# Two transformer layers on one core: the banks of the block products, weight places in halves, the fold of the weights, and the first loads

## The chip, the cores and the metric

The kernel runs on one core of one Trainium2 chip. The metric is the device time of one execution in microseconds (us). The engines of the core are PE (matrix products), PEld (PE's weight loads), DVE (vector), ACT (activations), POOL (GpSimd) and SP, which here issues every DMA. Each engine runs its own list of instructions in order, and semaphores tie the lists together.

## The reference

Two layers follow each other on `x` (16 batches of 256 rows by 256), all in float32. Each layer is self attention, cross attention and a feed-forward part, each with a layer norm that is scaled and shifted by a projection of the condition. Cut to what matters:

```python
# layer 0: 16 heads of 64 (rotary positions), width 1024; layer 1: 16 heads of 16, width 256
def layer(x, cond, context):
    h = norm(x) * (1 + cond @ g1) + cond @ b1
    x = x + attention(h, h)              # softmax(q k^T / sqrt(dh)) v, then @ wo
    h = norm(x) * (1 + cond @ g1) + cond @ b1   # layer 1 has its own three sets
    x = x + attention(h, norm(context))  # layer 1: context without the norm
    h = norm(x) * (1 + cond @ g2) + cond @ b2
    return x + gelu(h @ w1) @ w2         # 256 -> 1024 -> 256
```

The context has 256 rows by 192. In layer 1 the condition passes a silu first.

## The kernel before

The work is six phases (`p` = 0 to 5): self attention, cross attention and feed-forward of layer 0, then the same of layer 1. Each phase goes over 16 batches; a batch in a phase is a job. An attention job has two steps (`s` = 0, 1), a feed-forward job four. One loop over all steps issues everything, and the order in which a line of it stands in the program is the order on each engine; nothing is rescheduled. `x` stays in SBUF for all batches.

The PSUM has eight banks. In a layer 0 attention step the order on PE is:

- `stage_rotary` (L474) for the next step: the products of hT and cT with `wk` and `wq`. Unit e of the two uses banks 2e and 2e+1. DVE multiplies them by the rotary tables (`m`, L490), POOL combines these to `qk` (L498). A unit's `m` tiles have two places for each of two tags, so the second unit's `m` waits for POOL.
- `layer0_sums` (L594, products at L602): the weighted sums of the two units, in banks 4 and 5. ACT copies each bank to `raw` (L609).
- for `s` = 1, `finish_folded` (L702): the output projection of the batch before (`late`). It is one level of a block scheme with seven products of half-size blocks instead of eight; the blocks' sums of the hidden side are made in `fold_inner` (L693), those of the weights, once a phase, in `fold_weights` (L678). The products went to banks 1 and 0, DVE adds them to `x` in five instructions (L714 to L721).
- `layer0_values` (L424): the values of the next batch, in banks 6 and 7, copied out by ACT (L442).
- `scores` (L813), `stage_s` (L520): the score products of the next step, one unit in banks 0 to 3, then one in banks 4 to 7 (L533). ACT makes the exponentials (`pr`, L545) from them.
- for a cross attention step to come, `start_keys` (L462, product at L469), which reads `wk` for the step after.

DVE in a step adds the exponentials (`both`, L554), turns them (L560) and sums them (L567). In the next step `sum_up` (L569) sends the sums through DRAM to spread them (L579, L582); POOL multiplies `raw` with them (`scale`, L591) and makes three of the five hidden blocks' sums (L700), DVE the other two. Between the last `both` and the first of the next step DVE also prepares the norm of a batch to come.

The tiles of weights have places by tag: `wk`, `wq`, `wv`, `wo`, each with one place but `wo`. A phase's weights are fetched into them by `load_phase` (L789), in parts: "early" at batch 1 or 3 of the phase before, "values" at the start of that phase's last batch, "keys" at the end of the first step of that batch, after which `scores` calls `start_keys` on them. SP issues DMAs in the order of the program and stands still where one has to wait.

`idle_products` (L136) multiplies the identity with itself at the start, before the condition has been fetched.

Of the kernel before, what the change touches and what calls it, by code (L numbers as in the profile page):

```python
# [16 lines left out]
P = 128  # L17
N = 256
# [25 lines left out]
def fast(ctx: ExitStack, tc: tile.TileContext, a: dict, out: bass.AP, flag):  # L44
# [79 lines left out]
    nc.sync.dma_start(out=cond, in_=a["cond_1024"])  # L124
    load_x(0)
    nc.sync.dma_start(out=rows, in_=a["rows"])

    condT = const.tile([P, 2, KC, NB], F32, name="condT")
# [7 lines left out]
    def idle_products(n):  # L136

        for _ in range(n):
            nc.tensor.matmul(bank(0, P), ident, ident, start=True, stop=True)

    sig = work.tile([NB, D], F32, tag="inv", name="sig")
    nc.scalar.activation(sig, cond, AF.Sigmoid)
    soon = stat.tile([NB, 1], F32, tag="ve", name="soon")
    nc.scalar.activation(soon, cond[:, 0:1], AF.Exp)
    silu = work.tile([NB, D], F32, tag="inv", name="silu")
    idle_products(2)
    transpose_condition(0, cond)
    nc.vector.tensor_mul(silu, sig, cond)
    idle_products(2)
    transpose_condition(1, silu)  # L150
    idle_products(2)
    pr = bank(4, n_rows)
    nc.tensor.transpose(pr, rows, ident[:n_rows, :n_rows])
    idle_products(1)

    def load_modulation(shift_w, scale_w, name):
        w = wpool.tile([P, KC, 2, D], F32, tag="mod", name=f"mod_{name}", bufs=1)
        nc.sync.dma_start(out=w[:, :, 0, :], in_=shift_w.rearrange("(c p) m -> p c m", p=P))
        nc.sync.dma_start(out=w[:, :, 1, :], in_=scale_w.rearrange("(c p) m -> p c m", p=P))
        return w  # L160
# [23 lines left out]

    def layer0_modulation(i):
        w = load_modulation(a[f"L0_xcond_b{i}_w"], a[f"L0_xcond_g{i}_w"], f"a{i}")
        return lambda at: modulation(
            f"a{i}", at, 0, w,
            *(row_of[f"L0_xcond_{n}"][0] for n in (f"ln{i}_w", f"ln{i}_b", f"b{i}_b", f"g{i}_b")),
        )  # L190
# [23 lines left out]


    def load_layer0_attention(kind, part, between=None):
        halves = [slice(i * 512, (i + 1) * 512) for i in range(4)]
        wkv_src = chunked(a[f"{kind}_wkv"])
        w = {}
        if part == "keys":  # L220
            w["wk"] = wtile([P, 2, H * 64], "wk", f"wk_{kind}")
            w["wq"] = wtile([P, KC, H * 64], "wq", f"wq_{kind}")
            for i, cut in enumerate(halves[:2]):
                nc.sync.dma_start(out=w["wk"][:, :, cut], in_=wkv_src[:, :, cut])
                nc.sync.dma_start(out=w["wq"][:, :, cut], in_=chunked(a[f"{kind}_wq"])[:, :, cut])
                if between is not None and i == 0:
                    between()
# [22 lines left out]
    def load_layer1_cross(part):  # L250
        if part != "early":
            return {}
        w = wtile([P, 3, 2, D], "wk", "wqkv_c")
        nc.sync.dma_start(out=w[:, 0], in_=chunked(a["L1_xcond_Wq"]))
        nc.sync.dma_start(out=w[:, 1], in_=chunked(a["Wk_filled"]))
        nc.sync.dma_start(out=w[:, 2], in_=chunked(a["Wv_filled"]))
        wo = wtile([P, KC, D], "wo", "wo_b2", 2)
        nc.sync.dma_start(out=wo, in_=chunked(a["L1_xcond_Woc"]))
        return {"wq": w[:, 0], "wk": w[:, 1], "wv": w[:, 2], "wo": wo,
                "bo": broadcast_row(a["L1_xcond_boc"], "bo", "bo_b2"),  # L260
                "bv": broadcast_row(a["L1_xcond_bv"], "bv", "bv_b2"),
                "bq": lambda c: column("L1_xcond_bq", c), "bk": lambda c: column("L1_xcond_bk", c)}

    def load_ffn(w1n, w2n, b1n, b2n, key, part):
        if part == "keys":
            w1 = wtile([P, KC, 4 * D], "wq", f"w1_{key}")
            nc.sync.dma_start(out=w1, in_=chunked(a[w1n]))
            return {"w1": w1}
        if part == "early":
# [192 lines left out]
    def start_keys(job, u, at):  # L462


        for g in range(2):
            for half in range(2):
                col = (2 * u + half) * P + 64 * g
                r, m = slice(64 * half, 64 * half + 64), slice(64 * g, 64 * g + 64)
                nc.tensor.matmul(  # L469
                    bank(at + half, 2, N)[m, 1, :], job["phase"]["w"]["wk"][r, 1, col : col + 64],  # L470
                    job["kT"][r, 1, :], start=True, stop=False,
                )

    def stage_rotary(job, u, half, first_bank):  # L474


        w, key, cross = job["phase"]["w"], job["key"], job["cross"]
        at = (2 * u + half) * P
        pq = bank(first_bank + half, 2, N)
        for k in range(1 if cross else 2):  # L480
            product(
                pq[:, 1, :], w["wk"][:, k, at : at + P], job["kT"][:, k, :],
                k == 0 and not cross, k == 1 or cross,
            )
        for k in range(2):
            product(pq[:, 0, :], w["wq"][:, k, at : at + P], job["hT"][:, k, :], k == 0, k == 1)
        turns = []
# [167 lines left out]
    def ffn_hidden(job, u):  # L655
# [5 lines left out]
        for c in range(2):  # L661
            for k in range(KC):
                product(
                    ph[:, c, :], w["w1"][:, k, (2 * u + c) * P : (2 * u + c + 1) * P], job["hT"][:, k, :],
                    k == 0, k == KC - 1,
# [12 lines left out]
    def fold_weights(ph):  # L678
# [3 lines left out]
        for m, x, y, op in ((1, b[0][0], b[1][1], ALU.add), (3, b[0][1], b[1][1], ALU.subtract),  # L682
# [6 lines left out]
            else:  # L689
                folded[m] = work.tile([P, 4, P], F32, tag="qk", name=f"folded_w_{m}", bufs=4)  # L690
            (nc.gpsimd if ph["kind"] == "attn" and m < 4 else nc.vector).tensor_tensor(folded[m], x, y, op)

# [9 lines left out]
    def finish_folded(job, at):  # L702

        x, weights, hidden = xs[job["b"]], job["phase"]["folded"], job.pop("folded")
        final = job is jobs[-1]
        first, second, third = (bank(i, 4, P) for i in (at if final else (*at, at[1])))
        places = {5: first[:, 0], 2: first[:, 1], 4: first[:, 2], 3: first[:, 3],
                  1: third[:, 0], 7: second[:, 1], 6: second[:, 2]}
        for m in (3, 6, 4, 5, 2, 1, 7) if final else places:
            for c in range(4):  # L710
# [46 lines left out]
    def count_outside():  # L757
# [11 lines left out]
        {"layer": 0, "kind": "attn", "cross": False, "load": lambda part: load_layer0_attention("sa", part, load_first),  # L769
         "mod_load": lambda: layer0_modulation(1)},  # L770
        {"layer": 0, "kind": "attn", "cross": True, "load": lambda part: load_layer0_attention("ca", part), "mod_load": None},
# [59 lines left out]
    phases[0]["make_mod"] = phases[0]["mod_load"]()  # L831
    for part in ("keys", "early"):
        load_phase(0, part)
# [5 lines left out]


    jobs[0]["hraw"] = bank(7, KC, N)
    found = moments(xs[0], "first")
# [23 lines left out]
    for i, (j, s) in enumerate(steps):  # L866
# [10 lines left out]
        if s == 1 and job["b"] == (3 if ffn else 1) and more:  # L877
            load_phase(job["p"] + 1, "early")
        if s == 0 and job["b"] == NB - 1 and more:
            load_phase(job["p"] + 1, "values")  # L880
        if layer0 and not ffn and s == 1 and job["b"] == 2:
# [46 lines left out]
        elif layer0:  # L928
# [9 lines left out]
            if make_mod:  # L938
                make_mod["mod"] = make_mod["make_mod"](5)
            stage_t(job, 2 * s + 1, 1)  # L940
            rotary(then, 1, 0)
            if late is not None and s == 1:
                fold_inner(late, nc.vector, 7, 6)
            rotary(then, 1, 1)
            for e in range(2):
                layer0_sums(job, 2 * s + e, 4 + e if then else e)
# [3 lines left out]
            if late is not None and s == 1:  # L950
                finish_folded(late, (1, 0) if then else (7, 6))
            if late is not None and s == 0:
                scale(late)
                fold_inner(late, nc.gpsimd, 5, 2, 1)
            if s == 0 and job["b"] == 1:
                fold_weights(job["phase"])
            if nxt["kind"] == "attn":
# [5 lines left out]
            else:  # L963
                prepare_norm(third)
                prepare_context(third)
                prepare_input(after)
        else:
            then = attention(i + 1, 1)
# [15 lines left out]
            else:  # L984
                prepare_norm(third)
                prepare_input(after)
        if s == 0 and job["b"] == NB - 1 and more:
            load_phase(job["p"] + 1, "keys")
        scores(i + 1)
# [621 lines left out]
```

## The time and the profile before

| | us |
|---|---|
| three timed runs | 2240.68, 2245.42, 2246.43 (median 2245.42) |
| profiled execution, its own time | 2240.61 |
| its span, first to last instruction | 2238.8 |
| PE busy, share | 2192.0, 98% |
| DVE busy, share | 1721.4, 77% |
| ACT busy, share | 837.6, 37% |
| POOL busy, share | 998.4, 45% |

The profile follows one execution. "Busy" counts time in which an engine has an instruction under way; a wait is idle time of an engine just before an instruction, with what ended it. The granted clock of PE is told for a stretch of time (1.00 is full, 0.50 half). The line numbers in it are those of the code above.

By phase: the self attention of layer 0 lasts to about 660 us of the span, its cross attention to about 1330, its feed-forward part to about 1550; layer 1's two attentions follow to about 2017, and its feed-forward part to the end.

### The profile page before, as it was taken

What the parts mean: (1) busy time and instruction counts of PE and PEld (TensorE: products, weight loads), DVE (VectorE), ACT (ScalarE), POOL (GpSimd) and SP (SyncE); (2) the same over time, 40 slices, a digit from 0 to 9 for tenths busy, and PEclk for the clock granted to TensorE, in tenths of its full rate; (3) what the DMA queues carried; (4) which work ended last, traced back from release to release, by engine and by line L of the source; (5) the groups of instructions that cost most, each with busy time, mean ns of one, the idle gap of its engine ahead of it and who ended that gap; (6) DMA issues with size and microseconds to landing.
All of it is one profiled execution on the core that took longest, in us unless ns stands there. A gap on an engine that the chain in (4) does not pass through costs nothing.

```text
span 2238.8 us, 110884 instructions
## 1 busy us (share of the span) xinstructions
PE 2192.0 (98%) x50601; PEld 1446.6 (65%) x50601; DVE 1721.4 (77%) x3188; ACT 837.6 (37%) x1303; POOL 998.4 (45%) x970
## 2 busy tenths in 40 slices
PE   9999999999999899999999999999999999999998
PEld 5666666666656566666666668777656665656787
DVE  6888778788888899889988885564677777777654
ACT  2323332332332332333323332223566666663322
POOL 3656465465565566565665652211222222222120
PEclk9999999999999999999999999999999999999999
DMA  6210111111131321212212123221211232223221
GB/s 188 48 36 22 27 36 22 27 36 22 43 99 38 76 53 34 62 36 43 56 34 43 41 57 87 57 43 32 60 41 39 50 81 61 60 51 99 64 61 37
DMA packets 305703, 117.69 MB, mean 53 GB/s; under 512 B 242548, under 2 KB 288968, under 8 KB 305096
## 3 DMA queue, kind: packets, MB, share of 16 engines
q1 hardware_dynamic: 305224, 110.51, 20.6%
q8 instruction: 397, 6.50, 1.2%
q14 instruction: 82, 0.67, 0.1%
HBM read 77.14 MB, written 33.29 MB: 49 GB/s over the span
## 4 chain that ended last, share of the span: by engine, by line
PE 79%; POOL 7%; DVE 7%; DMA 3%; issue 2%; SPq 1%; ACT 0%; POOLq 0%; DVEq 0%; ACTq 0%
PE banks L82 53%; PE banks L533 14%; PE banks L602 6%; PE banks L618 5%; POOL raw L591 3%; DVE m L490 2%; POOL folded L700 2%; POOL qk L498 1%; DMA spread<-sums_seen 1%; DVE rows L567 1%; PE banks L469 1%; DMA sums_seen<-inv 1%; SPq L582 1%; DVE squares L560 1%; DVE folded L700 1%
## 5 line engine op out<-in xcount | busy, mean ns | idle before, releaser
L545 ACT ACTIVATE pr<-banks 128x1024 f32<-128x1024 f32 x576 | 487.4, 938 | 246.1 <-PE banks L533 220.9
L498 POOL TENSOR_TENSOR qk<-m,m 128x512 f32<-128x512 f32 x256 | 346.8, 1375 | 405.7 <-DVE m L490 272.3
L490 DVE TENSOR_TENSOR m<-banks,rope 128x512 f32<-128x512 f32 x512 | 325.8, 680 | 95.2 <-POOL qk L498 75.8
L554 DVE TENSOR_TENSOR both<-pr 128x512 f32<-128x512 f32 x256 | 236.7, 932 | 93.0 <-ACT pr L545 92.8
L533 PE MATMUL banks<-qk 32*64 32x256 f32 x8192 | 242.7, 379 | 21.9 <-DVE x L721 21.0
L533 PEld LDWEIGHTS banks<-qk 32*64 32x64 f32 x8192 | 192.1, 132 | 96.8 <-issue 51.5
L609 ACT COPY raw<-banks 128x512 f32<-128x512 f32 x128 | 75.1, 586 | 479.4 <-PE banks L602 479.4
L602 PE MATMUL banks<-pr,v 128*32 128x256 f32 x4096 | 233.4, 379 | 1.0 <-DVE add_a L182 1.0
L668 ACT ACTIVATE g<-banks,cols 128x256 f32<-128x256 f32 x256 | 107.0, 470 | 294.9 <-PE banks L82 275.7
L442 ACT COPY v<-banks 128x512 f32<-128x512 f32 x128 | 71.8, 587 | 336.8 <-PE banks L437 168.5
L602 PEld LDWEIGHTS banks<-pr,v 128*32 128x32 f32 x4096 | 132.9, 110 | 90.0 <-DVE add_a L182 1.5
L591 POOL TENSOR_TENSOR raw<-raw,spread 128x512 f32<-128x512 f32 x128 | 172.4, 1381 | 14.0 <-DMA spread<-sums_seen 13.3
L82 PE MATMUL banks<-folded_w,folded 128*32 128x128 f32 x5952 | 174.2, 273 | 0.0
L82 PEld LDWEIGHTS banks<-folded_w,folded 128*32 128x32 f32 x5952 | 163.9, 110 | 0.0
L560 DVE STREAM_TRANSPOSE squares<-both 128x1024 f32<-128x1024 f32 x128 | 159.4, 1246 | 4.4
L567 DVE TENSOR_REDUCE rows<-squares 128x32 f32<-128x1024 f32 x128 | 155.4, 1214 | 2.2
L653 POOL TENSOR_TENSOR oT<-oT,spread 128x256 f32<-128x256 f32 x64 | 45.7, 735 | 209.9 <-DVE spread L652 209.9
L296 POOL TENSOR_TENSOR rstd<-ve,neg_half 128x2 f32<-128x2 f32 x95 | 74.2, 781 | 142.1 <-DVE ve L294 138.8
L82 PE MATMUL banks<-hT,wk_sa 128*32 128x256 f32 x2048 | 136.4, 384 | 0.9 <-ACT hT L362 0.9
L618 PE MATMUL banks<-pr,wide_v 128*32 128x256 f32 x2048 | 134.4, 379 | 1.1 <-ACT pr L545 1.1
L700 POOL TENSOR_TENSOR folded<-raw,raw 128x512 f32<-128x512 f32 x93 | 134.0, 1467 | 2.4
L82 PE MATMUL banks<-hT,wq_sa 128*32 128x256 f32 x2048 | 134.8, 381 | 0.0
(156 smaller groups left out, 3626.2 us busy)
## 6 DMA issues: line engine op xcount, KB each, us to landing
turned<-blocks SPq DMA_DIRECT2D x380, 64.0 KB
fetched<-turned SPq DMA_DIRECT2D x380, 64.0 KB
spread<-sums_seen SPq DMA_DIRECT2D x128, 128.0 KB
x<-in_x SPq DMA_DIRECT2D x16, 256.0 KB
fetched_c<-turned_c SPq DMA_DIRECT2D x64, 64.0 KB
cT<-in_ctx_turned SPq DMA_DIRECT2D x16, 256.0 KB
out<-x SPq DMA_DIRECT2D x16, 256.0 KB
ctx<-in_ctx SPq DMA_DIRECT2D x16, 192.0 KB
```

The costliest lines, as they stand in the source:

```text
L82: nc.tensor.matmul(out[cut], lhsT[:, cut], rhs, start=start, stop=stop)
L490: nc.vector.tensor_tensor(m, pq, rope[:, s : s + 1, :].to_broadcast([P, 2, N]), ALU.mult)
L498: nc.gpsimd.tensor_tensor(r, x, y, (ALU.subtract, ALU.add)[out])
L533: nc.tensor.matmul(banks[64 * g : 64 * g + 64, at + h, t * N : (t + 1) * N], lhs, rhs, start=(half == 0), stop=(half == 1 or job["layer"] ...
L545: nc.scalar.activation(pr[:, one], sc[:, one], AF.Exp, scale=0.125 if job["layer"] == 0 else 0.25)
L554: nc.vector.tensor_tensor(job["both"][:, 2 * p : 2 * p + 2, :], pr[:, :, 0, :], pr[:, :, 1, :], ALU.add)
L560: nc.vector.transpose(job["squares"].rearrange("p b k -> p (b k)"), job.pop("both").rearrange("p h n -> p (h n)"))
L567: nc.vector.tensor_reduce(job["rows"][:, u, :], job.pop("squares"), AX.X, ALU.add)
L591: nc.gpsimd.tensor_tensor(part, part, spread[:, u : u + 1, :].to_broadcast([P, 2, N]), ALU.mult)
L602: nc.tensor.matmul(o[32 * h : 32 * h + 32, half, :], v[:, t, col : col + 32], prs[h // 2][:, h % 2, t, :], start=(t == 0), stop=(t == NT - 1),
L618: nc.tensor.matmul(o[32 * h : 32 * h + 32], v[:, t, 4 * c + h, 32 * e : 32 * e + 32], prs[h // 2][:, h % 2, t, :], start=(t == 0), stop=(t ...
L700: eng.tensor_tensor(folded[m], *sums[m])
```

## The change

- The block products of a layer 0 attention batch go to the banks of the weighted sums, 4 and 5, and no longer to 1 and 0. After the last attention step that has such products, they take three banks (7, 6, 5), in the order that only the very last batch had. The modulation that is made in such a step goes to bank 6, no longer 5.
- The places `wk` and `wq` become two places each, `wk0`, `wk1`, `wq0`, `wq1`. The first halves are fetched at the start of the last batch of a layer 0 attention phase, ahead of the values; the second halves after that step's last `stage_rotary`. The last feed-forward phase's `w1` is fetched at batch 1 of the phase before. The weights of layer 1's cross attention are laid into the new places.
- `fold_weights` of an attention phase is called at the end of the first batch (`s` = 1) and no longer in the first step of the second; all five blocks' sums are on POOL, where it was two on POOL and three on DVE.
- For the batch whose `finish_folded` falls in the last attention step, the three hidden blocks' sums that POOL made are made by DVE in that step.
- At the start `x` of batch 0 is fetched between the two halves of the modulation's weights, and the rows of vectors after them. The idle products have 256 columns in place of 128; there are five instead of seven.

The diff, cut to its core:

```diff
     def idle_products(n):
         for _ in range(n):
-            nc.tensor.matmul(bank(0, P), ident, ident, start=True, stop=True)
+            nc.tensor.matmul(
+                bank(0, 2, P), ident, ident.unsqueeze(1).to_broadcast([P, 2, P]), start=True, stop=True
+            )
...
-        if part == "keys":
-            w["wk"] = wtile([P, 2, H * 64], "wk", f"wk_{kind}")
-            w["wq"] = wtile([P, KC, H * 64], "wq", f"wq_{kind}")
...
+        if part in ("first", "last"):
+            i = ("first", "last").index(part)
+            wk, wq = (wtile([P, 2, 512], f"w{n}{i}", f"w{n}{i}_{kind}") for n in "kq")
+            nc.sync.dma_start(out=wk, in_=wkv_src[:, :, halves[i]])
+            nc.sync.dma_start(out=wq, in_=chunked(a[f"{kind}_wq"])[:, :, halves[i]])
+            w[f"wk{i}"], w[f"wq{i}"] = wk, wq
...
-            (nc.gpsimd if ph["kind"] == "attn" and m < 4 else nc.vector).tensor_tensor(folded[m], x, y, op)
+            (nc.gpsimd if ph["kind"] == "attn" else nc.vector).tensor_tensor(folded[m], x, y, op)
...
-        final = job is jobs[-1]
-        first, second, third = (bank(i, 4, P) for i in (at if final else (*at, at[1])))
+        hurry = len(at) == 3
+        first, second, third = (bank(i, 4, P) for i in (at if hurry else (*at, at[1])))
...
-        for m in (3, 6, 4, 5, 2, 1, 7) if final else places:
+        for m in (3, 6, 4, 5, 2, 1, 7) if hurry else places:
...
         if s == 1 and job["b"] == (3 if ffn else 1) and more:
             load_phase(job["p"] + 1, "early")
-        if s == 0 and job["b"] == NB - 1 and more:
-            load_phase(job["p"] + 1, "values")
+            if job["layer"] == 1:
+                for part in ("first", "last"):
+                    load_phase(job["p"] + 1, part)
+        leaving = layer0 and not ffn and job["b"] == NB - 1
+        if leaving and s == 0:
+            for part in ("first", "values"):
+                load_phase(job["p"] + 1, part)
...
             if make_mod:
-                make_mod["mod"] = make_mod["make_mod"](5)
+                make_mod["mod"] = make_mod["make_mod"](6)
             stage_t(job, 2 * s + 1, 1)
             rotary(then, 1, 0)
             if late is not None and s == 1:
-                fold_inner(late, nc.vector, 7, 6)
+                fold_inner(late, nc.vector, *((7, 6) if then else (6, 5, 2, 1, 7)))
             rotary(then, 1, 1)
+            if leaving and s == 0:
+                load_phase(job["p"] + 1, "last")
...
             if late is not None and s == 1:
-                finish_folded(late, (1, 0) if then else (7, 6))
+                finish_folded(late, (4, 5) if then else (7, 6, 5))
             if late is not None and s == 0:
                 scale(late)
-                fold_inner(late, nc.gpsimd, 5, 2, 1)
-            if s == 0 and job["b"] == 1:
-                fold_weights(job["phase"])
+                if nxt["kind"] == "attn":
+                    fold_inner(late, nc.gpsimd, 5, 2, 1)
...
                 prepare_input(after)
+                if job["b"] == 0:
+                    fold_weights(job["phase"])
...
-        if s == 0 and job["b"] == NB - 1 and more:
-            load_phase(job["p"] + 1, "keys")
         scores(i + 1)
```

More of the change, by code (lines that the diff above doesn't have):

```diff
@@ L124, in fast @@
     nc.sync.dma_start(out=cond, in_=a["cond_1024"])
-    load_x(0)
-    nc.sync.dma_start(out=rows, in_=a["rows"])
     condT = const.tile([P, 2, KC, NB], F32, name="condT")
@@ L138, in idle_products, with condition, load_modulation @@
         for _ in range(n):
-            nc.tensor.matmul(bank(0, P), ident, ident, start=True, stop=True)
[L141 to L156, printed above, removed]
+            nc.tensor.matmul(
+                bank(0, 2, P), ident, ident.unsqueeze(1).to_broadcast([P, 2, P]), start=True, stop=True
+            )
+    def condition():
+        sig = work.tile([NB, D], F32, tag="inv", name="sig")
+        nc.scalar.activation(sig, cond, AF.Sigmoid)
+        soon = stat.tile([NB, 1], F32, tag="ve", name="soon")
+        nc.scalar.activation(soon, cond[:, 0:1], AF.Exp)
+        silu = work.tile([NB, D], F32, tag="inv", name="silu")
+        idle_products(1)
+        transpose_condition(0, cond)
+        nc.vector.tensor_mul(silu, sig, cond)
+        idle_products(1)
+        transpose_condition(1, silu)
+        idle_products(2)
+        pr = bank(4, n_rows)
+        nc.tensor.transpose(pr, rows, ident[:n_rows, :n_rows])
+        idle_products(1)
+        return pr
+    def load_modulation(shift_w, scale_w, name, between=None):
         w = wpool.tile([P, KC, 2, D], F32, tag="mod", name=f"mod_{name}", bufs=1)
         nc.sync.dma_start(out=w[:, :, 0, :], in_=shift_w.rearrange("(c p) m -> p c m", p=P))
+        if between is not None:
+            between()
         nc.sync.dma_start(out=w[:, :, 1, :], in_=scale_w.rearrange("(c p) m -> p c m", p=P))
@@ L183, in modulation, with layer0_modulation @@
         return factor, addend
-    def layer0_modulation(i):
-        w = load_modulation(a[f"L0_xcond_b{i}_w"], a[f"L0_xcond_g{i}_w"], f"a{i}")
+    def layer0_modulation(i, between=None):
+        w = load_modulation(a[f"L0_xcond_b{i}_w"], a[f"L0_xcond_g{i}_w"], f"a{i}", between)
         return lambda at: modulation(
@@ L219, in load_layer0_attention @@
         w = {}
-        if part == "keys":
-            w["wk"] = wtile([P, 2, H * 64], "wk", f"wk_{kind}")
-            w["wq"] = wtile([P, KC, H * 64], "wq", f"wq_{kind}")
[L223 to L227, printed above, removed]
+        if part in ("first", "last"):
[4 more added lines that the diff above has]
+            w[f"wk{i}"], w[f"wq{i}"] = wk, wq
+            if between is not None and i == 0:
+                between()
         if part == "values":
@@ L252, in load_layer1_cross @@
             return {}
[L253 to L256, printed above, removed]
+        wqk = wtile([P, 2, 2, D], "wk0", "wqk_c")
+        nc.sync.dma_start(out=wqk[:, 0], in_=chunked(a["L1_xcond_Wq"]))
+        nc.sync.dma_start(out=wqk[:, 1], in_=chunked(a["Wk_filled"]))
+        wv = wtile([P, 2, D], "wk1", "wv_c")
+        nc.sync.dma_start(out=wv, in_=chunked(a["Wv_filled"]))
         wo = wtile([P, KC, D], "wo", "wo_b2", 2)
         nc.sync.dma_start(out=wo, in_=chunked(a["L1_xcond_Woc"]))
-        return {"wq": w[:, 0], "wk": w[:, 1], "wv": w[:, 2], "wo": wo,
+        return {"wq": wqk[:, 0], "wk": wqk[:, 1], "wv": wv, "wo": wo,
                 "bo": broadcast_row(a["L1_xcond_boc"], "bo", "bo_b2"),
@@ L264, in load_ffn @@
     def load_ffn(w1n, w2n, b1n, b2n, key, part):
[L265 to L268, printed above, removed]
+        if part in ("first", "last"):
+            i = ("first", "last").index(part)
+            w1 = wtile([P, KC, 2 * D], f"wq{i}", f"w1{i}_{key}")
+            nc.sync.dma_start(out=w1, in_=chunked(a[w1n])[:, :, i * 2 * D : (i + 1) * 2 * D])
+            return {f"w1{i}": w1}
         if part == "early":
@@ L466, in start_keys @@
             for half in range(2):
-                col = (2 * u + half) * P + 64 * g
+                col = (2 * (u % 2) + half) * P + 64 * g
                 r, m = slice(64 * half, 64 * half + 64), slice(64 * g, 64 * g + 64)
                 nc.tensor.matmul(
-                    bank(at + half, 2, N)[m, 1, :], job["phase"]["w"]["wk"][r, 1, col : col + 64],
+                    bank(at + half, 2, N)[m, 1, :], job["phase"]["w"][f"wk{u // 2}"][r, 1, col : col + 64],
                     job["kT"][r, 1, :], start=True, stop=False,
@@ L477, in stage_rotary @@
         w, key, cross = job["phase"]["w"], job["key"], job["cross"]
-        at = (2 * u + half) * P
+        at = (2 * (u % 2) + half) * P
         pq = bank(first_bank + half, 2, N)
@@ L481, in stage_rotary @@
             product(
-                pq[:, 1, :], w["wk"][:, k, at : at + P], job["kT"][:, k, :],
+                pq[:, 1, :], w[f"wk{u // 2}"][:, k, at : at + P], job["kT"][:, k, :],
                 k == 0 and not cross, k == 1 or cross,
@@ L485, in stage_rotary @@
         for k in range(2):
-            product(pq[:, 0, :], w["wq"][:, k, at : at + P], job["hT"][:, k, :], k == 0, k == 1)
+            product(pq[:, 0, :], w[f"wq{u // 2}"][:, k, at : at + P], job["hT"][:, k, :], k == 0, k == 1)
         turns = []
@@ L663, in ffn_hidden @@
                 product(
-                    ph[:, c, :], w["w1"][:, k, (2 * u + c) * P : (2 * u + c + 1) * P], job["hT"][:, k, :],
+                    ph[:, c, :], w[f"w1{u // 2}"][:, k, (2 * (u % 2) + c) * P : (2 * (u % 2) + c + 1) * P], job["hT"][:, k, :],
                     k == 0, k == KC - 1,
@@ L769, in fast @@
         {"layer": 0, "kind": "attn", "cross": False, "load": lambda part: load_layer0_attention("sa", part, load_first),
-         "mod_load": lambda: layer0_modulation(1)},
+         "mod_load": lambda: layer0_modulation(1, lambda: load_x(0))},
         {"layer": 0, "kind": "attn", "cross": True, "load": lambda part: load_layer0_attention("ca", part), "mod_load": None},
@@ L831, in fast @@
     phases[0]["make_mod"] = phases[0]["mod_load"]()
-    for part in ("keys", "early"):
+    nc.sync.dma_start(out=rows, in_=a["rows"])
+    for part in ("first", "last", "early"):
         load_phase(0, part)
@@ L835, in fast @@
         load_x(b)
+    pr = condition()
     jobs[0]["hraw"] = bank(7, KC, N)
```

## The prediction

> **What bounds the kernel now.** First the page: PE is busy for 98% of the span, so no more than 47 us of waits are there to be had, unless PE is slow while it is busy.
>
> ```profile
> PE 2192.0 (98%) x50601; PEld 1446.6 (65%) x50601; DVE 1721.4 (77%) x3188; ACT 837.6 (37%) x1303; POOL 998.4 (45%) x970
> ```
>
> Then the list of waits, PE's lines alone (who waits, for whom: us in total, times, longest).
>
> ```profile
> PE banks L533 <- DVE x L721: 21.0, 15, 2.8
> PE banks L469 <- DMA wk_ca<-in_ca_wkv: 4.7, 1, 4.7
> PE banks L82 <- DMA w_b<-in_L_xcond_W: 3.2, 1, 3.2
> PE banks L82 <- POOL rstd_c L296: 2.3, 1, 2.3
> PE banks L82 <- POOL folded L700: 2.2, 2, 1.6
> PE banks L602 <- DVE add_a L182: 1.0, 1, 1.0
> ```
>
> The edits aim at these. The largest is the scores' wait for DVE's last addition to x. The same list over 60 to 650 us has 0.7 us of it, over 688 to 1300 us 20.4 us: it belongs to layer 0's cross attention. Whether PE gains it depends on DVE, so the third view is what DVE itself waits for in that stretch.
>
> ```profile
> DVE m L490 <- POOL qk L498: 36.6, 29, 2.5
> DVE both L554 <- ACT pr L545: 14.3, 32, 2.0
> DVE m L490 <- PE banks L82: 7.9, 15, 1.6
> ```
>
> The second and third line are DVE waiting for PE's scores and products: together 22.2 us. The first is the shape of the rotary (unit two's `m` needs POOL's `qk` of unit one) and stays. The windows (us, then busy time of PE, PEld, DVE, ACT, POOL, the granted clock of PE, DMA share and GB/s) show the steps, and PE's clock after three waits.
>
> ```profile
> 892.86:910.19 17.33, 16.25 (x338) 9.56 (x337) 15.05 (x26) 7.00 (x10) 7.90 (x8) 1.00 0.38 82
> 910.19:932.58 22.39, 22.39 (x556) 15.23 (x552) 20.98 (x33) 6.02 (x8) 17.11 (x14) 1.00 0.07 18
> 814.50:830.76 16.26, 16.26 (x341) 9.19 (x337) 13.67 (x23) 6.93 (x10) 7.78 (x8) 1.00 0.41 91
> 668.53:671.93 3.40, 3.03 (x28) 1.48 (x32) 0.00 (x0) 0.00 (x0) 3.32 (x4) 0.50 0.99 347
> 1177.11:1180.52 3.41, 3.41 (x79) 3.10 (x67) 2.22 (x6) 1.67 (x2) 1.90 (x4) 0.50 0.28 45
> 1323.89:1327.29 3.40, 3.38 (x64) 3.14 (x68) 3.40 (x4) 0.00 (x0) 2.75 (x2) 0.50 0.02 5
> ```
>
> A cross batch is a step of 17.33 and one of 22.39 us; without the wait the first would be 16.26. In the second DVE works 20.98 of 22.39 us. Last, rows of one timeline (start, us, engine, line), around one such wait.
>
> ```profile
> 919.14 1.79 DVE L554 TENSOR_TENSOR both<-pr 128x512 f32<-128x512 f32 x1
> 922.07 0.59 ACT L609 COPY raw<-banks 128x512 f32<-128x512 f32 x1 [5.99 <-PE banks L602]
> 923.55 1.93 PE L82 MATMUL banks<-wo_ca,folded 128*32 128x128 f32 x64
> 933.20 0.42 DVE L721 TENSOR_TENSOR x<-banks,x 128x256 f32<-128x256 f32 x1
> 933.77 4.43 PE L533 MATMUL banks<-qk 32*64 32x256 f32 x128 [1.19 <-DVE x L721]
> 935.87 1.94 ACT L545 ACTIVATE pr<-banks 128x1024 f32<-128x1024 f32 x2 [1.18 <-issue]
> ```
>
> **Banks 4 and 5.** Nothing is added or removed; what changes is who waits. Unit one's scores (banks 0 to 3) no longer wait for the additions; unit two's (4 to 7) do. A unit is half of 128 records in 3.71 us, so the additions get 1.86 us more. The waits, mostly 0.9 to 1.6 us, would vanish at today's DVE timing. PE would gain 20.4 us plus 1.7 us, because the half clock at 1177 follows one of these waits. But PE then runs ahead of DVE: a batch costs PE 16.26+22.39=38.65 us, and DVE 39.72 less the waits it can lose. In the batch shown these are 0.65 us on ACT and 0.28 on PE, so DVE needs 38.79. The two are nearly equal, and once PE's lead of 1.86 us is used up DVE sets the pace. Over the phase DVE can give 22.2 us; I take that. The new neighbour is the copy of bank 4, which must be out before the first block product: it ends at 922.66, the product starts at 923.55. Bank 5 is needed two rows of 1.93 us later. Both cost nothing. Late next: L721 before unit two.
>
> **The fold of the weights.** In the cross phase three DVE instructions of 1.48 us (mean of that row) go: +4.4. Five on POOL at its 1.47 (L700's row) are 7.4 us. POOL stands idle for 6.60 us between cT and its next `qk` (896.9 to 903.5), so `qk` comes 0.8 later. Beside them run DVE's `both`. Alone one takes 0.69; the row at 919.14, next to POOL's blocks' sums, took 1.79. [...] I take the trace: 4.4-2.0-0.8=+1.6. PE's 2.3 us (put down to rstd_c) lies in the same batch and is DVE's or POOL's lateness, so it isn't counted again. In the self phase DVE has cover; there it is worth the 0.7 wait and a little: 1.0.
>
> **Weights in halves.** `wk_ca` was issued at 664.4 and PE stood still for 4.7 us, then ran 3.4 us at half clock (1.7 lost, of which some 1.5 in products). PE's side: 6.2. SP's queue: two DMAs (1 MB) now pass the values, the context, the sums and four spreads; two more pass eight fetches. At the 347 GB/s of the 668.53 row, 2 MB take 6.0 us from 649.1 on, and the values are used at 657.7: a wait of 0 to 1.3. The sums' DMA stands behind them, so `spread`, which POOL already waited 3.5 us for here, comes 1 to 2 us later; then raw, blocks' sums, `qk`, and DVE's second `m`, which was at 677.9. I get 676.4 without a late spread and 677.9 with one. DVE's side thus gains 0 to 1.5: 0.7, and DVE's side counts, as the phase behind it is DVE's. Fetching `w1` a phase sooner: all of the 3.2.
>
> **Clock.** [...] By the trace the dips cost 3x1.7=5.1. I use the trace, on PE's side only.
>
> **End of the cross phase.** PE waited 1.65+0.59 for POOL's blocks' sums and then ran 3.4 us at half clock: 3.9 on PE's side. Now DVE makes five at 0.70: its `both` end near 1322.5 (3.31 for two, less the contention), the first sum at 1323.2. From there six products of 0.94 us end at 1328.9, where they ended at 1331.0: +2.1. The modulation's bank: the 1.0 us wait goes, inside DVE's pace.
>
> **First loads.** Not shown before, so bounded. Idle products: 0.61 us each for 128 columns (1.23 for two at half clock); 256 columns cost 0.61 to 1.22, five of them 3.1 to 6.1 against 4.3; I take 4.5, near the mean. The rows of vectors land after 768 KB and stand before the modulation in PE's order: up to 1.3 late. For: the first products (16 records) took 1.94 us at 11.5 and 1.04 from 16.6, half clock, 2.5 us lost; denser products may get full clock sooner. Ends -1.3 and +3.2; I take +1.0.
>
> **Sum.** 22.2+1.6+1.0+0.7+3.2+2.1+1.0=31.8. Against the profiled execution, 2240.61 (span 2238.8 and 1.8 around it), that is 2208.8: 2209. The median, 2245.42, lies 4.8 higher; the three runs spread over 5.8, so the range leans upward.
>
> **Rivals.**
> - PE sets the pace all through. For: every edit meets a PE wait. 20.4+1.7+2.3+1.0 in the cross phase, 6.2, 3.9, 3.2, start and self phase 2: 40.7, so 2200. Against: 20.98 of 22.39.
> - Contention eats the cross phase: POOL's instructions meet more of DVE's, and the wait for L721 comes back at unit two. What stays is PE's lead 1.9, half of the recoverable 22.2 lost: 2240.6-20.6 is 2220; if nearly all of it is lost, 2228.
> - Slower: the copies of banks 4 and 5 (L609) come late and hold the block products in all 31 batches. The slack is 0.89 us. To undo 31.8 us and lose 0.3% (6.7), each must wait 1.24, so the copy must come 2.1 us later than now; at 2.5 later it is 31x1.61=50 more, 2259. Against: ACT was idle 5.99 us before the copy.
> - The change does not do what it says: PE meets another wait right behind L721 (`qk`, ready 3.5 us before in the batch shown), and only loads and ends count: 2238 to 2246.
>
> **How the numbers follow.** A measurement of this kernel tells about 0.3% from no change, 6.7 us. Likeliest case 0.62 (alone 2202 to 2217); PE's pace 0.18; contention 0.12; no effect 0.05; slower 0.03. Faster: 0.62+0.18+0.12=0.92. The range reaches from below PE's pace, 2197, to 2226; left out are the slower case, no effect and the worst of contention and start, under 0.2.
>
> **What would show it.** L533's wait for L721 under 6 us in all; L469's and `w_b`'s gone; DVE's waits for `pr` and PE in the cross phase under 6 us, with the one for `qk` near 36; cross batches near 38.8 us; half clock at most once after the start. Wrong: a wait of L82 for `raw` L609, or cross batches at 39.5 with DVE without waits.

## The result and the profile after

The changed kernel takes 2213.14 us (median of four runs, 2212.19 to 2216.62) beside 2245.93 us for the kernel before (2240.68 to 2246.55): a ratio of 0.9862, with a 95% interval of 0.9843 to 0.9880. Run again beside the last two experiments it took 2211.99 us against 2242.09, 0.9864 (0.9849 to 0.9880). Its profiled execution took 2212.19 us (span 2210.4). The line numbers of the changed kernel are those of before plus 7 around the steps: L533 is now L540, L545 L552, L554 L561, L490 L497, L498 L505, L591 L598, L700 L707, L714 to L721 are L721 to L728.

The page's row of busy times, and PE's part of the list of waits (who waits, for whom: us in total, times, longest):

```profile
PE 2190.7 (99%) x50597; PEld 1431.3 (65%) x50597; DVE 1705.5 (77%) x3185; ACT 838.3 (38%) x1303; POOL 1005.2 (45%) x973
```

```profile
PE banks L82 <- DVE folded L707: 3.8, 2, 2.8
PE banks L540 <- DVE x L728: 2.2, 7, 0.3
PE banks L540 <- DVE x L724: 1.0, 3, 0.3
PE banks L82 <- ACT hT L369: 1.4, 1, 1.4
```

Of the six waits shown of before, those for `wk_ca`, `w_b`, `rstd_c` and `add_a` are gone, and the one for the last addition to `x` went from 21.0 to 2.2 us; 1.0 us of waits for the third addition (L724) is new. The one for POOL's `folded` (2.2) is now one for DVE's, and longer. DVE's own waits in the cross phase (681.3 to 1273 us):

```profile
DVE m L497 <- POOL qk L505: 47.4, 30, 4.3
DVE m L497 <- PE banks L82: 0.6, 2, 0.3
DVE both L561 <- ACT pr L552: 0.2, 1, 0.2
```

Here is the surprise. The 22.2 us that DVE spent waiting for PE and `pr` are down to 0.8, as foreseen; but the wait for POOL's `qk`, which I took as fixed at 36.6 us, is 47.4.

**A wait that the list does not show.** In this trace a hold between the two units' scores can lie partly inside a row's busy time. The timeline (start, us, engine, line) of one first step of a batch, in the changed kernel, and of the same step in the last experiment below, where nothing holds it:

```profile
1074.73 2.71 PE L540 MATMUL banks<-qk 32*64 32x256 f32 x66
1077.75 1.98 PE L540 MATMUL banks<-qk 32*64 32x256 f32 x62 [0.31 <-DVE x L728]
1079.66 1.09 PE L476 MATMUL banks<-cT,wk_ca 64*64 64x256 f32 x16
```

```profile
1074.08 3.86 PE L555 MATMUL banks<-qk 32*64 32x256 f32 x128
1077.86 1.09 PE L491 MATMUL banks<-cT,wk_ca 64*64 64x256 f32 x16
```

From the first score product to the first product of another kind it is 4.93 us in the one and 3.78 in the other: 1.15 us lost where the list counts 0.31. The records of the first row reach past unit one's 64. So I count the length of the score blocks, each with the wait in front of it: over the 29 steps from the start of the cross phase, what they take above 3.64 us, the shortest, is 23.3 us before (19.4 of it in front) and 12.2 after (nothing in front). The wait moved to unit two, smaller, as "late next" had it, and did not vanish.

**Where the time went.** The starts of the same steps in both profiles give the saving by stretch (us):

| stretch | before | after | saved | foreseen |
|---|---|---|---|---|
| to the third scores | 64.11 | 61.70 | 2.4 | 1.0 (first loads) |
| to the last self attention step | 596.39 | 595.97 | 0.4 | 1.0 (fold), values 0 |
| from there to the 30th of 32 cross steps | 614.51 | 593.91 | 20.6 | 24.5 (22.2+1.6+0.7) |
| from there to the first `w_a` product | 55.80 | 53.46 | 2.3 | 2.1 |
| to the first `w_b` product | 690.89 | 688.03 | 2.9 | 3.2 |
| to the end | 217.1 | 217.3 | -0.2 | 0 |
| sum | 2238.8 | 2210.4 | 28.4 | 31.8 |

### The profile page after: what moved, and what is told of

Read it like the earlier page. It is cut to its first block, busy times and chain, and to the rows that moved or that the text cites. A ratio compares the mean times of both kernels' runs of the same rounds, so it can differ in the third digit from the quotient of the medians.

```text
span 2210.4 us, 110913 instructions
## 1 busy us (share of the span) xinstructions
PE 2190.7 (99%) x50597; PEld 1431.3 (65%) x50597; DVE 1705.5 (77%) x3185; ACT 838.3 (38%) x1303; POOL 1005.2 (45%) x973
## 4 chain that ended last, share of the span: by engine, by line
PE 91%; DVE 3%; POOL 2%; DMA 1%; issue 1%; SPq 0%; ACT 0%; DVEq 0%; POOLq 0%; ACTq 0%
PE banks L82 60%; PE banks L540 15%; PE banks L609 9%; PE banks L625 5%; PE banks L476 1%; PE banks L444 1%; DVE m L497 1%; POOL raw L598 1%; POOL qk L505 0%; DMA sums_seen<-inv 0%; POOL folded L707 0%; DMA spread<-sums_seen 0%; PE banks L175 0%; DVE both L561 0%; DVE folded L707 0%
## 5 line engine op out<-in xcount | busy, mean ns | idle before, releaser
L552 ACT ACTIVATE pr<-banks 128x1024 f32<-128x1024 f32 x576 | 488.4, 936 | 229.5 <-PE banks L540 212.1
L505 POOL TENSOR_TENSOR qk<-m,m 128x512 f32<-128x512 f32 x256 | 345.3, 1368 | 364.5 <-DVE m L497 244.8
L497 DVE TENSOR_TENSOR m<-banks,rope 128x512 f32<-128x512 f32 x512 | 325.1, 678 | 99.0 <-POOL qk L505 94.3
L561 DVE TENSOR_TENSOR both<-pr 128x512 f32<-128x512 f32 x256 | 233.4, 923 | 80.1 <-ACT pr L552 79.7
L540 PE MATMUL banks<-qk 32*64 32x256 f32 x8192 | 246.6, 378 | 3.9 <-DVE x L728 2.2
L540 PEld LDWEIGHTS banks<-qk 32*64 32x64 f32 x8192 | 184.6, 131 | 89.3 <-issue 23.0
L598 POOL TENSOR_TENSOR raw<-raw,spread 128x512 f32<-128x512 f32 x128 | 172.8, 1383 | 18.0 <-DMA spread<-sums_seen 11.4
L82 PE MATMUL banks<-hT,wq_ca 128*32 128x256 f32 x2048 | 134.0, 379 | 0.0
```

What stands on the lines that cost most here:

```text
L82: nc.tensor.matmul(out[cut], lhsT[:, cut], rhs, start=start, stop=stop)
L497: nc.vector.tensor_tensor(m, pq, rope[:, s : s + 1, :].to_broadcast([P, 2, N]), ALU.mult)
L505: nc.gpsimd.tensor_tensor(r, x, y, (ALU.subtract, ALU.add)[out])
L540: nc.tensor.matmul(banks[64 * g : 64 * g + 64, at + h, t * N : (t + 1) * N], lhs, rhs, start=(half == 0), stop=(half == 1 or job["layer"] ...
L552: nc.scalar.activation(pr[:, one], sc[:, one], AF.Exp, scale=0.125 if job["layer"] == 0 else 0.25)
L561: nc.vector.tensor_tensor(job["both"][:, 2 * p : 2 * p + 2, :], pr[:, :, 0, :], pr[:, :, 1, :], ALU.add)
```

## The experiments

Each was timed in turns with the kernel before; ratios are to that kernel. Three chips were used, on which the kernel before took 2240.5 (the first four), 2241.5 (the next four) and 2242.1 us (the last three), so times of different groups are compared by ratio or by stretches of the profile. The changed kernel itself was not run beside the first eight, and the kernel before took 2245.9 us beside its first timing: ratios of different groups can differ by some 0.2% for that alone. Differences of a few us from the changed kernel are therefore read from the profiles, of one execution each.

**Banks alone.** The kernel before, with one part of the change.

```diff
-                make_mod["mod"] = make_mod["make_mod"](5)
+                make_mod["mod"] = make_mod["make_mod"](6)
...
-                finish_folded(late, (1, 0) if then else (7, 6))
+                finish_folded(late, (4, 5) if then else (7, 6))
```

> The kernel before with one edit: block products in banks 4 and 5, the modulation in bank 6. DVE's pace (the theory): DVE's waits for pr and PE in the cross phase, 22.2 us before, nearly go, PE's wait for L721 falls from 21 to under 4, and PE is at most one unit of scores (1.9) ahead; the weights' fold stays on DVE. 18 to 21 us less than before: 2225 to 2228. PE's pace: 20.4+1.7+1.0 less, 2223, and DVE would keep idle time in every batch. If the waits only move to another place: under 8 us less, over 2238.

Measured: 2219.76 us, 0.9919 (0.9902 to 0.9936), 20.7 us less. In the profile the stretch across the cross phase is 596.41 us, 18.1 saved of the 20.6, and the score blocks lose 7.1 us in place of 23.3. Nearly the whole gain of that stretch is in two bank numbers. DVE's wait for `qk` over 681.3 to 1273 us grew only a little, from 36.6:

```profile
DVE m L490 <- POOL qk L498: 39.8, 30, 3.7
```

**Banks undone.** The changed kernel with the block products back in banks 1 and 0 and the modulation in bank 5.

> The changed kernel with the block products back in banks 1 and 0 and the modulation in bank 5 (the last step keeps its three banks). DVE's pace: DVE again waits some 20 us for pr and PE, PE some 17 us for the last addition to x; 16 to 20 us over the changed kernel: 2229 to 2233. If the other edits had made the room (a lighter DVE): under 10 over it.

Measured: 2235.23 us, 0.9974 (0.9964 to 0.9985), 2 us above the expected range. PE's waits, then DVE's in its cross phase:

```profile
PE banks L540 <- DVE x L728: 24.1, 15, 3.2
```

```profile
DVE m L497 <- POOL qk L505: 37.5, 27, 3.1
DVE both L561 <- ACT pr L552: 18.6, 30, 2.2
DVE m L497 <- PE banks L82: 7.2, 14, 1.4
```

All three old waits are back, and `qk` is at its old size. Without the banks the other edits are worth 0.26%. Six windows of 3.41 us at half clock fell into the stretch up to its 30th cross step, where before had two (granted clock 0.98 from 684.49 to 1279.25 us; before had 1.00 from 688.96 to 1275.01). But the profiled execution was the slowest of the eight (2239.61 us), so they tell why it was slow; why the median lies above the range stays open.

**Halves fetched late.** The changed kernel, first and last halves at the end of the step, where `keys` stood.

```diff
-            for part in ("first", "values"):
-                load_phase(job["p"] + 1, part)
+            load_phase(job["p"] + 1, "values")
...
-            if leaving and s == 0:
-                load_phase(job["p"] + 1, "last")
...
+        if leaving and s == 0:
+            for part in ("first", "last"):
+                load_phase(job["p"] + 1, part)
         scores(i + 1)
```

> The changed kernel with both halves of the weights fetched where the kernel before did, at the end of the last batch's first step; the places stay in halves. PE stands still at start_keys again for some 4.7 us and may fall to half clock. DVE's pace: the phase behind it is DVE's, and DVE loses only 0 to 1.5 us by the late fetch, so 0 to 2.5 us over the changed kernel: 2213 to 2216. PE's pace: the wait and the half clock come back whole, 4.7 to 6.2 more: 2218 to 2219.

Measured: 2214.37 us, 0.9893 (0.9877 to 0.9910); span 2210.3, that of the changed kernel.

```profile
PE banks L476 <- DMA wk_ca<-in_ca_wkv: 4.7, 1, 4.7
```

PE stood still for 4.7 us again, with a window at half clock (mean granted clock of the span 0.998, of the changed kernel's 0.999), and in the profile it cost nothing that lasts: across the cross phase 594.17 us against 593.91, and the score blocks lost 7.4 us in place of 12.2. What PE loses there it would otherwise have lost to DVE behind it. This speaks for "DVE's pace" and against "PE's pace" (6.2 us more). The times do not decide it: the profiled execution was the fastest of its four (2212.21 to 2217.91 us), and the ratio is 0.3% above that of the changed kernel, which was not timed beside it.

**Fold undone.** The changed kernel with `fold_weights` in the first step of the second batch, two on POOL and three on DVE.

> The changed kernel with the weights' fold where and on which engines it was (first step of batch 1, two sums on POOL, three on DVE). By the trace's contention: 1.6 in the cross phase, under 1.0 in the self phase: 1.6 to 2.6 over the changed kernel, 2215 to 2216. If each vector addition beside the five POOL instructions had waited a whole one: 2.3 less in the cross phase, so 2211 to 2212.

Measured: 2214.98 us, 0.9890 (0.9873 to 0.9906). In the profile the self phase is no longer than with the change (595.96 us against 595.97): what the kernel before lost there is won back by the banks alone, too (595.37 us, and 596.39 before). The cross stretch is 592.69 us, against 593.91, 593.06, 592.96 and 593.80 in the four profiles with the new fold: the edit brought nothing there.

Its price had been put about right. In the changed kernel, beside POOL's five sums (7.58 us), DVE's four `both` took 2.55+1.80+0.62=4.97 us, where four alone take 2.76: 2.2 lost. The prediction's 2.0 was twice what two in a row lost in the profile of before, next to POOL's `raw` (2.36 in place of 1.38):

```profile
1316.12 4.72 POOL L591 TENSOR_TENSOR raw<-raw,spread 128x512 f32<-128x512 f32 x3
1317.34 2.36 DVE L554 TENSOR_TENSOR both<-pr 128x512 f32<-128x512 f32 x2
```

The other case of the expectation, that each of the four waits for a whole sum on POOL (1.47 us by the prediction, 5.9 in all: 4.4-5.9-0.8=-2.3), did not come. The single instructions in the changed kernel:

```profile
726.23 1.71 POOL L698 TENSOR_TENSOR folded_w<-wo_ca 128x512 f32<-128x512 f32 x1
726.73 1.77 DVE L561 TENSOR_TENSOR both<-pr 128x512 f32<-128x512 f32 x1
```

The second `both` began while POOL's first sum ran, and ended 0.56 us after it; the third took 1.80 us, and ended 0.55 us after POOL's fourth. Each of the two took 1.1 us longer than the 0.69 of one alone, a little less than POOL's fourth sum lasted (1.28 us). The first, which had begun ahead of POOL's sums, took 0.86, and the fourth, behind them, 0.62. So 5.9 was too large because two of the four lost 1.1 each, the first 0.17 and the fourth nothing.

With three DVE sums of 1.47 us back, PE waited 2.3 us once for `folded` and then ran a window at half clock (mean granted clock of the span 0.998), but the score blocks lost 6.8 us in place of 12.2. As with the halves fetched late, PE lost less to DVE later; that the one makes up for the other fits both runs, and was not tested by itself.

**Start undone.** First loads and idle products as before.

> The changed kernel with the first loads in the old order and seven idle products of 128 columns. The first scores began at 26.6 us in place of 27.9, and the first step was 1.1 shorter; both come back: 1.3 to 2.4 over the changed kernel, 2214 to 2216, with the first products of rotary at half clock until about 16.6. If the clock depends on where its window falls, and not on these edits: within 1 of the changed kernel.

Measured: 2213.11 us, 0.9868 (0.9845 to 0.9890): no difference from the changed kernel's 0.9862 and 0.9864. The third scores start at 62.89 us, inside the 61.40 to 65.52 of the nine profiles with the new start.

**End undone.** The last batch's three blocks' sums on POOL again.

> The changed kernel with the last folded batch of the cross phase as before: POOL makes three of its five sums, two banks, old order. The changed kernel waits 2.77 us there for DVE, without half clock. Theory: 2.1 over the changed kernel, from POOL's lateness (1.7+0.6) and half clock after it if that returns; 0.3 to 2.3 over it, 2213 to 2215.5. If DVE's five sums cost as much as POOL's three: 0.

Measured: 2215.74 us, 0.9885 (0.9861 to 0.9909), which overlaps the changed kernel's interval. From the 30th cross step to `w_a` it took 53.41 us, the changed kernel 53.46 and, run again, 52.61. So the 2.3 us of the table cannot be called the edit's: before had a half clock there (0.50 from 1323.88 to 1327.29 us), and this kernel, with POOL's sums again and a wait of 1.91+0.59 us for them, had none (mean granted clock of the span 0.999, of before 0.997).

**Blocks left out.** In the cross phase DVE's two hidden blocks' sums are left out (plain blocks stand in), two instructions of 0.68 us a batch.

```diff
-                fold_inner(late, nc.vector, *((7, 6) if then else (6, 5, 2, 1, 7)))
+                if late["p"] == 1 and then:
+                    halves = late["halves"]
+                    late["folded"].update({7: halves[1][:, :, 0:P], 6: halves[0][:, :, P : 2 * P]})
+                else:
+                    fold_inner(late, nc.vector, *((7, 6) if then else (6, 5, 2, 1, 7)))
```

> The changed kernel, in the cross phase without DVE's two blocks' sums per batch (a plain block takes the place of each; the output is not the reference's). This takes 1.28 us per batch from DVE and nothing from PE. DVE's pace: cross batches fall from 39.3 us on average to PE's 38.6, about 9 us less than the changed kernel: 2202 to 2206. PE's pace: within 1.5 of it.

Measured: 2205.98 us, 0.9838 (0.9816 to 0.9860), span 2202.2. PE's work is the same, the score blocks lose 3.2 us in place of 12.2, and from the fourth batch on every cross batch takes 38.6 us, PE's own pace. So DVE's work lay on the path that set the pace of what was left.

**Turned inputs written later.** Why is POOL's `qk` late? Its `raw` (L598) stands ahead of it and needs the sums, which go through DRAM by two DMAs. In a batch near the middle the sums are issued at 1007.74 and the spreads, which wait for their landing, at 1010.28:

```profile
1000.28 2.99 SPq L326 DMA_DIRECT2D turned<-blocks  x4
1003.70 2.54 SPq L349 DMA_DIRECT2D turned_c<-blocks_c  x4
...
1007.74 0.34 SPq L586 DMA_DIRECT2D sums_seen<-inv  x1
1010.28 1.74 SPq L589 DMA_DIRECT2D spread<-sums_seen  x4
```

that is 2.54 us, where the same batch of before took 2.03 and an undisturbed one takes 1.48. Ahead of it on SP are the writes of the turned inputs for a later batch. In most batches of before they were issued 8.5 to 9.2 us ahead of the sums, in this batch 8.9; now it is 7.5 in most, because the step is shorter. In the rows of windows (last two columns: DMA share, GB/s), the stretch just ahead of the sums is full of them, as it was before (0.46):

```profile
1003.87:1007.74 3.87, 3.87 (x84) 2.40 (x80) 3.87 (x8) 0.00 (x0) 0.12 (x1) 1.00 0.48 79
```

So the writes of the cross phase were put behind the sums' DMAs (cut; those of the context in the same way):

```diff
     def turn(xh, nb, name):
...
+        def write():
             for g in range(4):
                 nc.sync.dma_start(out=turned[:, :, g, :], ...)
+        held.append(write) if holding[0] else write()
...
     def prepare_fetch(job):
+        release()
...
+                holding[0] = job["p"] == 1 and job["b"] < NB - 1
                 prepare_norm(third)
                 prepare_context(third)
+                holding[0] = False
```

> The changed kernel with the DMA writes of the turned blocks in the cross phase issued after the sums' DMAs of the next step, not before them. DVE waits 47.4 us for POOL's qk in the cross phase, 36.6 before; in those batches the sums' DMA takes 2.2 to 3.5 us to land, and POOL's raw starts late. Theory (the sums' DMA stands behind the turned blocks' writes): it lands in about 1.5 us everywhere, the wait for qk falls to about 37, and 5 to 9 us less: 2204 to 2208. If the lateness comes from elsewhere (the spreads themselves, POOL's own work): within 1.5 of the changed kernel. If the fetch then comes late for hT: slower.

Measured: 2208.87 us, 0.9848 (0.9826 to 0.9870). The same stretch ahead of the sums, and DVE's wait in the cross phase:

```profile
1006.00:1009.87 3.87, 3.87 (x84) 2.39 (x80) 3.87 (x8) 0.00 (x0) 0.12 (x1) 1.00 0.02 4
```

```profile
DVE m L512 <- POOL qk L520: 37.1, 29, 4.3
```

The spreads now go out 1.47 to 1.55 us after the sums in nine of sixteen batches (three of sixteen in the changed kernel), the wait for `qk` is at its old 37 us, the score blocks lose 6.6 us, and the cross stretch is 588.59 us, 5.3 less. So the writes ahead of the sums cost time, and without them the cross stretch gains what was missing. Two things stay open. In the tenth to the fourteenth of the sixteen batches the spreads still went out 1.8 to 3.0 us after the sums, with no turned inputs written ahead; in four of the five a fetch of instructions of 16 KB was under way (the profile's instruction queue has 397 packets, 6.50 MB), and whether it is the cause was not tested. And that the shorter step is what made the transfer later is not shown: with the banks undone the writes lay 8.5 us or more ahead, and the spreads went out up to 3.4 us after the sums all the same.

**The changed kernel again, the later writes again, and a filled start.** The third puts three idle products behind the first transposes:

```diff
                 jobs[0]["hraw"][:, c, t * P : (t + 1) * P], xh[:, t, c * P : (c + 1) * P], ident
             )
+    idle_products(3)
     prepare_input(jobs[0])
```

> The changed kernel as it is, beside the next two on one chip, so that they can be set against it. Expected: 0.985 to 0.988 of the kernel before. Its profile is read for the start: in the profiles so far the same start gave first scores between 26.3 and 29.3 us. If that is chance (a clock whose windows of 3.41 us run free of the kernel), this one falls anywhere between; if it belongs to each kernel's code, it gives 26.6 again.

> The changed kernel with the writes of the turned inputs put behind the sums' transfers in the cross phase, again. Theory (transfers queued ahead of the sums hold up GpSimd's scaling, and DVE with it): from the last step of the self phase to step 61 about 588.6 us as in its first profile, against 593.9 of the changed kernel, so some 4 to 5 us under the changed kernel's time on the same chip, 0.983 to 0.985 of the kernel before. Rival (its first time was a matter of the chip or the start): no more than 1 us from the changed kernel's time.

> As the one before, and three products on the identity, 256 columns each, behind the transposes of the first normalized input, where PE stood 0.9 to 1.4 us waiting for ACT's first hT. Theory (a standing PE gives the half clock to the window behind it): the first L82 products run at full clock, two groups of 1.93 us become 1.04 us, and one window of half clock at most is left behind 10 us; the filling costs up to 0.8 us; so 1 to 2 us less than the one before. Rival (the half clock at the start has other grounds, such as products of few columns): 0 to 0.8 us more.

Measured: 2211.99 us (2210.74 to 2213.25), 0.9864; 2208.81 (2206.84 to 2212.53), 0.9857 (0.9841 to 0.9872); 2207.43 (2204.89 to 2209.32), 0.9849 (0.9836 to 0.9863). On one chip the later writes take 3.2 us off the changed kernel, a little under the 4 to 5 expected; intervals overlap, while the cross stretch (593.80, 590.15 and 588.44 us) shows where it is. With the filled start the first products of the rotary run at full clock in its one profile (1.00 from 9.33 to 11.20 us). The timelines of the changed kernel again and of the filled start:

```profile
10.90 1.94 PE L82 MATMUL banks<-hT,wk_sa 128*32 128x256 f32 x16 [1.37 <-ACT hT L369]
12.60 1.93 PE L82 MATMUL banks<-hT,wq_sa 128*32 128x256 f32 x16
14.31 1.93 PE L82 MATMUL banks<-hT,wk_sa 128*32 128x256 f32 x16
```

```profile
9.65 1.46 PE L136 MATMUL banks<-ident 128*128 128x256 f32 x6
11.18 1.22 PE L82 MATMUL banks<-hT,wk_sa 128*32 128x256 f32 x16
12.22 1.05 PE L82 MATMUL banks<-hT,wq_sa 128*32 128x256 f32 x16
```

Its first scores start at 25.24 us, the later writes' at 26.51 and the changed kernel's at 27.63. The 1.4 us between the medians of the two last kernels is what was expected, but lies inside their scatter. The later writes with the filled start is the best version seen that computes the reference: 4.6 us under the changed kernel on that chip, by the medians.

## Why the prediction was right, point by point

- **Sum.** 31.8 us were foreseen; the spans differ by 28.4 and the medians by 32.8. The time (2209) was 4 us under the median measured, inside the range.
- **Banks 4 and 5: right in kind, 22.2 too large.** The cross stretch gained 20.6 us of 24.5, and 18.1 with the banks alone. That DVE's waits for PE and `pr` go was right (22.2 to 0.8), and that DVE then sets the pace too: in the profile a PE wait of 4.7 us brought back costs nothing, and DVE work taken out shortens the cross stretch by 9 us.

  The step that failed is "the first is the shape of the rotary and stays": that term of 36.6 us grew to 47.4. It is not only a shape; it ends with POOL, and POOL hangs on a transfer. In the cross phase POOL's `raw` waited 2.7 us for the spread before, 7.3 after and 2.2 with the later writes, and its four instructions took 5.5 to 6.0 us in most batches, where before had 5.0 to 5.5. Of the 10.8 us of waiting, the later writes give 10.3 back, but only 5.3 us of time: over the same steps DVE's busy time rose from 515.67 to 521.11 us, so a sum of waits is not a gain.

  Nor do the banks by themselves make all of the 10.8: the wait was 39.8 us with the banks alone, 40.4 with the halves fetched late and 39.8 with the fold undone. These three are the kernels with the new banks in which PE stood still for 2.3 to 5.4 us early in the phase; in the changed kernel (47.4, and 46.9 again), the start undone (43.7) and the end undone (45.0) it did not. That a PE which lost nothing there runs ahead of DVE and POOL sooner would fit; it was not tested. Cross batches took 39.3 us from the fifth on, in place of 38.8; this sign and `qk` near 36 did not come.
- **The fold of the weights: not found.** The contention was priced well: no run shows the 2.0 itself, which doubles the 0.98 us that two `both` lost in the profile of before, and the four of the changed kernel lost 2.2. But the phase is no shorter for the edit, where +1.6 was taken; and in the self phase the 1.0 is the banks' as much as the fold's, so it was counted in an edit that isn't needed for it.
- **Weights in halves: right by the profiles.** DVE's side counts there, not PE's 6.2. The 0.7 can't be told from nothing (593.91 against 594.17). The `w_b` wait of 3.2 gave 2.9.
- **Clock.** No half clock came behind the start, as foreseen (1.00 from 14.32 to 2209.09 us), but this was in part luck: PE now stood still for 2.77 us at the end of the cross phase, and the fold undone, with a wait of 2.8 us for `folded`, had a half clock there (0.50 from 1301.10 to 1304.50). The length of a wait alone does not tell it: in the profile of before the 3.21 us ahead of `w_b` left full clock, and half clock followed the 2.13 us just ahead of 1177 us. What stood beside it is below.
- **End of the cross phase.** 2.3 measured, 2.1 foreseen, which is luck: PE waited 2.77 us for DVE's sums, longer than the 1.65+0.59 for POOL's that should go, and the experiment gives the edit none of it for certain. Some 1.7 us (half of 3.41) is the half clock that before happened to have.
- **First loads.** +1.0 was taken, 2.4 stands in the table, and the experiment shows nothing: by that, chance of the clock in that execution (half from 10.91 to 14.32 us in the changed kernel's profile).
- **Rivals.** Full contention (2220) came in part. What an experiment shows of it came another way than told, by DMAs ahead of DMAs; how much of it is POOL beside DVE was not tested. The block products never waited for the copies of banks 4 and 5: in the cross phase bank 4 was out 0.89 us ahead of them in every batch. The sign "L533's wait under 6 us" was too weak: the list has 3.2, the score blocks 12.2.

## What to carry to other kernels

When two engines need nearly the same time for a batch (here PE 38.65 and DVE 38.79 us, by the prediction's estimate), removing one's waits can hand the pace to the other, and every wait of that other which "stays" has to be followed to its source: it can end with a transfer on another engine's path, as the 47.4 us for `qk` did in part. Issue the small transfer that someone waits for ahead of the large ones that nobody needs yet: here sums of 16 KB stood behind four writes of 64 KB and four of 48 KB, and the cross stretch took 5.3 us less when they went first. And measure a hold by the distance between the starts of two groups, since the list of waits can show a quarter of it (3.2 us of 12.2 here).

## What the runs showed of the hardware

In these runs the half clock does not follow the length of a wait. In the clock records of the profile of before, the stretches at full clock between two half ones, 505.17 and 143.36 us, are 148 and 42 times 3.413 us, the 651.95 ahead of them is 191 times that, and each of the three half clocks lasted 3.41 us. So both profiles can be laid out in windows of 3.413 us. Against the start of the span these lie differently: one begins at 16.58 us in the profile of before and one at 7.49 in that of the changed kernel, 2.66 windows apart.

What stood beside the half clock is PE's idle time within one such window. In the profile of before, 21 of the 630 windows between 30 and 2180 us have over 0.9 us of it. Three of them, from 665.11, 1173.69 and 1320.47 us, have 3.41, 2.13 and 2.22 us, and half clock followed each. The next have 1.82 and 1.74 us, and full clock went on; so it did behind the two windows over which the wait of 3.21 us for `w_b` falls, with 1.71 and 1.50. In the changed kernel the window with most, over the same stretch, has 2.05 us, and full clock went on. Whether a value between 2.05 and 2.13 decides, or something else does, these profiles do not show.

That window of the changed kernel holds part of a wait of 2.77 us for `folded`; the fold undone has a wait of 2.8 us there, with 2.44 us idle in one window. The two, and the window behind the second (the granted clock is the column after POOL):

```profile
1297.73:1301.14 3.41, 1.36 (x52) 1.36 (x56) 3.31 (x6) 0.00 (x0) 0.00 (x0) 1.00 0.03 7
```

```profile
1297.70:1301.10 3.40, 0.96 (x28) 0.69 (x22) 3.26 (x5) 1.08 (x2) 0.95 (x1) 1.00 0.00 0
1301.10:1304.50 3.40, 3.08 (x60) 2.85 (x64) 3.40 (x6) 0.00 (x0) 0.00 (x0) 0.50 0.02 5
```

PE was busy for 1.36 us of the first, and full clock went on; for 0.96 of the second, and half clock followed. So in these two nearly the same wait was followed by 3.41 us at half clock, 1.7 us by my estimate (half of 3.41), or by none. In the first 30 us the idle time alone does not tell it: in the changed kernel PE was busy for 2.22 of the 3.42 us from 7.49, so 1.20 idle, and half clock followed. And at the start the same code gave its first scores at 26.56 us in one profile of the changed kernel and at 27.63 in the other, and anywhere between 26.3 and 29.3 over the profiles with it. A single profile can't tell an edit there that is worth less than that.
